# Graph-attention plus relational attention on one core: four reorderings of VectorE and TensorE work

## The chip, the core and the metric

The kernel runs on one core of a Trainium2 chip. A core has a matrix engine (TensorE, "PE" in the profile; its weight loads are listed apart as "PEld"), three engines for elementwise work (VectorE or DVE, ScalarE or ACT, GpSimd or POOL) and SyncE (SP), which here only issues DMAs. Each engine works through its own list of instructions in order and waits on semaphores for the others. The metric is the device time of one execution in microseconds (us).

## The reference

The input is `x` of shape (64, 256, 256), float32: 64 graphs of 256 nodes with 256 features, and `adj`, (64, 256, 256), int32. Two layers follow each other. Everything is float32.

```python
# layer 0: two graph attentions, then a feed-forward block
def _gat(h, adj, W, a, out_features):
    Wh = jnp.matmul(h, W)
    Wh1 = jnp.matmul(Wh, a[:out_features])
    Wh2 = jnp.matmul(Wh, a[out_features:])
    e = Wh1 + jnp.swapaxes(Wh2, 1, 2)
    e = jax.nn.leaky_relu(e, negative_slope=ALPHA)
    scores = jnp.where(adj > 0, e, NEG)
    att = jax.nn.softmax(scores, axis=1)
    return jnp.matmul(att, Wh)
...
h = _gat(x, adj, W1, a1, Fout)
h = _gat(h, adj, W2, a2, W2.shape[1])
h = _layernorm(residual + h, g_ln1, b_ln1)
ff = jnp.matmul(jax.nn.relu(jnp.matmul(h, w_ff1) + b_ff1), w_ff2) + b_ff2
return _layernorm(residual2 + ff, g_ln2, b_ln2)

# layer 1: attention of 8 heads with 32 features each, values by relation, then feed-forward
scores = jnp.einsum('bhid,bhjd->bhij', q, k) / np.sqrt(dh)
attn = jax.nn.softmax(scores, axis=-1)
for r in range(Wv.shape[0]):
    v_r = (src @ Wv[r] + bv[r]).reshape(Bb, Nn, h, dh).transpose(0, 2, 1, 3)
    mask = (adj_matrix == r)[:, None]
    out = out + jnp.einsum('bhij,bhjd->bhid', attn * mask, v_r)
x = _ln(src + attn_out, g1, beta1)
ff = jax.nn.gelu(x @ W1 + b1, approximate=False) @ W2 + b2
return _ln(x + ff, g2, beta2)
```

The hidden width of both feed-forward blocks is 1024.

## The kernel before

Two graphs form a group (512 rows), and the 64 graphs are 32 groups. After a prologue (weights are folded, the first two groups' graph attention and the first feed-forward block of group 0 are done), `turn(u, u+1, u+2)` runs for u = 0 to 31. One turn interleaves three groups at different places of the pipeline: `Y` (group u) does its relational attention and its second feed-forward block, `X` (group u+1) its first feed-forward block, `Z` (group u+2) both graph attentions. Turns 30 and 31 have no `Z`, turn 31 has no `X` either.

Inside `tc.manual_schedule` the engines named there take their instructions in the order in which the Python code emits them: TensorE, SyncE, VectorE and ScalarE in turns with an `X`, TensorE and SyncE alone in turn 31 and in the prologue. GpSimd's order, and what is not named, is left to a scheduler. PSUM, the accumulator that TensorE writes, has eight banks: six are handed out in turn by `bank`, and two ("po", "zo") hold sums of the attention and, earlier in the turn, products of the values.

Large matrix products are split in quarters and done with seven products in place of eight. In each of them the results 1 and 2 go to one quarter of the output, 6 and 3 to another, 5 and 7 to the third, and 4 to the last. What comes first for a quarter is copied out of PSUM by ScalarE, what comes second is added by VectorE. Products 2, 5, 3 share one bank, each on top of the last, and 1, 6, 7, 4 another. So each product waits until the copy or addition of the one before it in its bank has read the bank. There are three of these:

- `Projections` (called as `p("q2 v2 ...")`): queries and keys ("q") and values ("v") of the attention. Copies stand at line 1036, additions at line 1040.
- `hidden_seven` (called as `first("6a")` or `second("2a 1a")`): the 1024 hidden features. Each step is done for two halves, a and b. Products stand at line 898 (tiles h1a and h1b), copies at 907, additions at 910, the activation functions at 916 (steps c, d, s and 4) and 941 (step r). The first product of the second operand needs differences of the input, `tt`, line 881.
- `HiddenOut` (called as `out(1)`): back to 256 features, added into the rows `y`. `product` (line 987, tile yf) and `add` (line 995) can be called apart. `sums` (line 973, tiles eq and eaq) makes the sums of hidden features that products 5, 6, 3 and 7 take.

The names that matter in a turn, in the order of the code:

- `scores`, `powers`, `masks`, `totals` and `sums` do the attention in four parts (two graphs by two sets of four heads). `scores` is the product (tile sp, line 1073), `powers` the exponentials (line 1082, tile e), `masks` multiplies them by the relation's mask (line 1086, tile ea, two instructions of 1024 columns), `totals` adds over a block (line 1091, tile es), and `sums` runs the products po and zo (lines 1101, 1104). zo needs es.
- `normed_features` turns normalised rows into features: four transpositions of 32x32 blocks on VectorE (line 694, tile yt), then sixteen moves across partitions, twelve by DMA and four by GpSimd (lines 711 and 713, or 703; tile hT).
- `early(z)` transposes the rows of group u+2 (line 1128, tile xT, one instruction of 1024 columns). Its readers are the products xpp (line 740).
- `norm` takes the moments (lines 826 and 827) and GpSimd's power of -1/2 (lines 837 and 838, tile rs). `offsets` (line 845, tile nm) is VectorE's small product of mean and rs, and `applied_norm` is ScalarE's scaling of the rows (line 855), four instructions for 512 rows. If `applied_norm` gets no list of rows, it calls `offsets` first.
- `Softmax` (tiles s and z) is the graph attention: `scores` (lines 766 and 768), `exp` (771), `masks` (775, two instructions for each graph) and `shares` (779, the reciprocal z). `scaled` (791) needs z. `first_sums` (line 800, tile hpp) follows.
- `divided` (lines 1112 to 1117) divides the attention by its totals; it is called by `shares(b)` of `turn`.

Of the kernel before, what the change touches and what calls it, by code (L numbers as in the profile page):

```python
# [12 lines left out]
ALU = mybir.AluOpType  # L13
# [372 lines left out]
def narrow_path(  # L386
# [482 lines left out]
    def hidden_seven(u, l, hT, w, bi, func, d, tt):  # L869

        a11, a12, a22, s1, s2, s3, s4 = w
        quarter = [[hT[k][:, b * NB:(b + 1) * NB] for b in range(G)] for k in range(KB)]

        def moving(n):
            return tt[:, n * N:(n + 1) * N].rearrange("p (t a r) -> p t a r", t=NB, r=32)

        def sub(n, x_, y_):  # L880
            nc.vector.tensor_tensor(moving(n), x_, y_, ALU.subtract)  # L881

        sub(0, quarter[0][1], quarter[0][0])
# [4 lines left out]
        one, two = ([None, None] for _ in halves)  # L888

        def out(h, o, b):  # L890

            f = o * FB // 2 + 2 * h
            return d["h1"][:, f:f + 2, b * N:(b + 1) * N]

        def product(ps, h, w_, m, first):
            for i in range(2):
                f = 2 * h + i
                nc.tensor.matmul(ps[:, i * N:(i + 1) * N], w_[:, f * P:(f + 1) * P], m,  # L898
                                 start=first and i == 0, stop=True,
                                 skip_group_check=True)  # L900

        def pair(ps):
            return ps.rearrange("p (f n) -> p f n", f=2)

        def copied(h, o, b, ps):

            mark["copied"] = nc.scalar.copy(out(h, o, b), pair(ps))  # L907

        def added(h, o, b, ps):
            mark["added"] = nc.vector.tensor_tensor(out(h, o, b), pair(ps), out(h, o, b), ALU.add)  # L910

        def done(h, o, b, ps=None):
            for i in range(2):
                f = o * FB // 2 + 2 * h + i
                y = d["h1"][:, f, b * N:(b + 1) * N]
                nc.scalar.activation(y, y if ps is None else ps[:, i * N:(i + 1) * N], func,  # L916
                                     bias=bi[:, f:f + 1])

        def step(name):
            n, h = name[0], "ab".index(name[1])  # L920
            if n == "2":
                two[h] = bank(f"h1b{u}_{l}_{h}")
                product(two[h], h, a12, quarter[1][0], True)
                copied(h, 0, 0, two[h])
            elif n == "1":
                one[h] = bank(f"h1a{u}_{l}_{h}")
                product(one[h], h, a11, quarter[0][0], True)
                added(h, 0, 0, one[h])
            elif n == "5":
                product(two[h], h, s1, moving(0), True)  # L930
                copied(h, 1, 1, two[h])
                mark["fifth"] = mark["copied"]
            elif n == "3":
                product(two[h], h, s4, quarter[1][1], False)
                added(h, 0, 1, two[h])
            elif n == "6":
                product(one[h], h, s2, moving(1), False)
                copied(h, 0, 1, one[h])
            elif n == "r":
                for f in range(2 * h, 2 * h + 2):  # L940
                    nc.scalar.activation(d["h1"][:, f, :], d["h1"][:, f, :], func, bias=bi[:, f:f + 1])
            elif n == "7":
                product(one[h], h, s3, moving(2), False)
                added(h, 1, 1, one[h])
# [61 lines left out]
    class Projections:  # L1006
# [3 lines left out]
        def __init__(s, u, hT):  # L1010
            s.u = u
            s.qk = work.tile([P, KB, 2, TN], F32, tag="q", name=f"qk{u}", bufs=1)
            s.v = work.tile([P, T, 2 * F], F32, tag="v", name=f"v{u}", bufs=1)
            s.h = [[hT[k][:, b * N:(b + 1) * N] for b in range(G)] for k in range(KB)]
            s.one, s.two = {}, {}

        def sums(s):
            tt = work.tile([P, HPB, NB * N], F32, tag="e", name=f"tq{s.u}").rearrange("p a n -> p (a n)")
# [13 lines left out]
            tag = ("zo", "po")[n]  # L1032
            return psum.tile([P, 512], F32, tag=tag, name=f"v{n}_{s.u}")

        def copied(s, x, o, b, ps):
            nc.scalar.copy(s.out(x, o, b), ps.rearrange("p (i n) -> p i n", i=2))  # L1036

        def added(s, x, o, b, ps):
            y = s.out(x, o, b)
            mark["projected"] = nc.vector.tensor_tensor(y, ps.rearrange("p (i n) -> p i n", i=2), y, ALU.add)  # L1040

        def step(s, x, n):
            a11, a12, a22, s1, s2, s3, s4 = wqks if x == "q" else wvs
# [9 lines left out]
                nc.tensor.matmul(ps[:, i * N:(i + 1) * N], l, r, start=n in (1, 2, 5) and i == 0, stop=True,  # L1053
                                 skip_group_check=True)
            to = {1: (0, 0), 2: (0, 0), 5: (1, 1), 6: (0, 1), 3: (0, 1), 7: (1, 1), 4: (1, 0)}[n]
            (s.added if n in (1, 3, 7) else s.copied)(x, *to, ps)

        def __call__(s, names):
            for n in names.split():
# [155 lines left out]
    def turn(y_, x_, z):  # L1215
# [46 lines left out]
        with order:  # L1262
            p.sums()
            if X:
                n = X.pop("n")
                offsets(*n)
            p("q2 v2 q1 v1")
            if X:
                applied_norm(X["y"], *n, [0, 1, 2, 3])
                X["hT"] = normed_features(x_, 0, X["y"])  # L1270
            p("q5")
            scores(0, (0, 1))
# [5 lines left out]
            p("v5 q6")  # L1278
            powers(0, (2,))
            p("v6")  # L1280
            powers(0, (3,))
            if X:
                masks(0)
            p("q3 q7")
            p("v7")
            if X:
                totals(0)
            else:
                with behind("projected"):
                    masks(0)  # L1290
                    totals(0)
            p("v3 q4 v4")
            steps = first_hidden(x_) if X else None
            if waiting:
                last = norm(w, 3, wy, mv=last)
# [3 lines left out]
                offsets(*last)  # L1299
            masks(1, (2,))  # L1300
            totals(1)
            if Z:
                early(z)
            sums(0)
            if waiting:
                first("2a 1a")
                applied_norm(wy, *last, [0, 1])
                first("5a")
                applied_norm(wy, *last, [2, 3])
            else:  # L1310
                first("2a 1a 5a", 1)
            scores(2)
            sums(1)
            first("6a")
# [55 lines left out]
            if Z:  # L1370
                out(1)
                Z["m"].scores(0)
                Z["m"].scores(1)
                Z["m"].exp(0)
                Z["m"].exp(1)
                out.sums(4)
                out(2, 5)
            elif X:
                out(5)
                out.sums(3)  # L1380
            applied_norm(y, *n)
# [42 lines left out]
            second("2a 1a")  # L1424
            if X:
                n = norm(x_, 1, X["y"], mv=n, rest=range(NB + 1, T))
            second("2b 1b ca 6a")
            if X:
# [3 lines left out]
            second("5a")  # L1432
            if X:
                applied_norm(X["y"], *n, [1])
            if Z:
                affine(y, rg3, rb3)
            second("6b 5b cb")
            if Z:
                X["hT"] = normed_features(x_, 1, X["y"], natural=True)
            second("7a 7b sa sb 3a da 3b db 4a 4b")  # L1440
            if X and not Z:
                affine(y, rg3, rb3)
                X["hT"] = with_ones(to_features(X["y"], f"h2T{x_}", (nc.vector.tensor_copy,) * 2))
            if y_ >= NG - 2:
                pieces = out_pieces(y_, y, h1)
                if X:
# [36 lines left out]
    with tc.manual_schedule(engines={mybir.EngineType.PE, mybir.EngineType.SP}):  # L1483
# [90 lines left out]
```

## Time and profile before

| | |
|---|---|
| median of three runs | 3062.04 us (3059.02 to 3063.88) |
| the profiled execution | 3056.92 us |
| its span, first to last instruction | 3055.3 us |
| mean granted TensorE clock | 0.994 of full speed |
| SyncE's DMA queue q1 | 418,076 packets, 102.20 MB, 15.3% of 16 engines |

A turn (but the last, 85 us) takes 91 to 95 us, measured from one group's first projection difference to the next one's. In the 40 slices of the profile TensorE is at 90% or more in all but the first and the last. A matmul in the trace overlaps the next one, so a busy TensorE row hides short waits; the rows of the weight loads (PEld) show them. In these lines, the number in brackets is the idle time of the engine before the first instruction of the row, with what ended it. The chain of waits gives, for each piece, its start, its length and its place; the table of waits gives who waited for whom, the sum in us, how often, and the longest.

### The profile page before, as it was taken

The page shows a single profiled execution, that of the slowest core. Times are in us where ns is not written, and L with a number is a line of the kernel's source. Part 1 is how long each engine was busy: PE and PEld are TensorE (multiplying, and loading weights), DVE is VectorE, ACT ScalarE, POOL GpSimd, SP SyncE. Part 2 cuts the span into 40 slices and gives each one's busy share as a digit, 9 for nine tenths or more (in the row PEclk, how much of TensorE's full clock was granted, in tenths as well). Part 3 has the DMA queues.
Part 4 walks back from the last instruction along what each step waited for, and adds up shares of the span by engine and source line. Part 5 has one row for each costly group of instructions (what it writes and reads, how often), then busy time and mean ns, then how long its engine had stood idle before and what let it go on. Part 6 is the DMA issues. An engine that isn't in the chain of part 4 may idle for free.

```text
span 3055.3 us, 58545 instructions
## 1 busy us (share of the span) xinstructions
PE 2966.2 (97%) x22192; PEld 2496.0 (82%) x22192; DVE 2614.3 (86%) x5025; ACT 1718.4 (56%) x3562; POOL 638.3 (21%) x930
## 2 busy tenths in 40 slices
PE   7999999999999999999999999999999999999997
PEld 5788888888888888888888888888888887888876
DVE  4788888889888889898889888898888888988876
ACT  4455555655655655555556556555556555555553
POOL 4222111221211222211222212222112212112211
PEclk8999999999999999999999999999999999999999
DMA  5011111211111211111111112111112111111000
GB/s 147 13 31 39 37 38 25 44 37 39 37 33 32 44 37 39 34 27 41 42 37 39 34 25 44 37 40 37 39 25 44 37 39 34 28 39 37 24 8 16
DMA packets 428405, 113.26 MB, mean 37 GB/s; under 512 B 364587, under 2 KB 427605, under 8 KB 428117
## 3 DMA queue, kind: packets, MB, share of 16 engines
q1 hardware_dynamic: 418076, 102.20, 15.3%
q10 hardware_dynamic: 8984, 6.19, 0.8%
q8 instruction: 178, 2.92, 0.4%
q0 software_dynamic: 1056, 1.05, 0.1%
q14 instruction: 111, 0.90, 0.1%
HBM read 56.78 MB, written 16.78 MB: 24 GB/s over the span
## 4 chain that ended last, share of the span: by engine, by line
PE 67%; DVE 17%; SPq 6%; DMA 3%; POOL 3%; issue 2%; ACT 1%; ACTq 0%; DVEq 0%; POOLq 0%
PE yf L987 21%; PE h1a L898 13%; PE h1b L898 9%; SPq L713 6%; PE po L1101 4%; PE xpp L740 4%; PE yop L811 4%; PE ygp L811 3%; DVE yt L694 3%; PE qk L1053 2%; DMA hT<-yt 2%; PE v L1053 2%; DVE s L775 2%; DVE tt L881 2%; PE sp L1073 1%
## 5 line engine op out<-in xcount | busy, mean ns | idle before, releaser
L1086 DVE TENSOR_TENSOR ea<-e,aT 128x1024 f32<-128x1024 f32 x256 | 308.0, 1215 | 54.5 <-ACT e L1082 54.5
L855 ACT ACTIVATE y<-y,nm,rs 128x256 f32<-128x256 f32 x450 | 242.6, 593 | 163.0 <-DVE nm L845 158.3
L1082 ACT ACTIVATE e<-sp 128x512 f32<-128x512 f32 x512 | 270.5, 597 | 27.7 <-PE sp L1073 21.0
L907 ACT COPY h<-h1b 128x512 f32<-128x512 f32 x256 | 149.0, 582 | 214.2 <-PE h1b L898 206.3
L837 POOL TENSOR_SCALAR rs<-mv 128x4 f32<-128x4 f32 (+1 forms) x134 | 56.3, 420 | 963.7 <-DVE mv L827 833.7
L1036 ACT COPY qk<-qk 128x512 f32<-128x512 f32 x128 | 74.5, 582 | 317.0 <-PE qk L1053 316.9
L916 ACT ACTIVATE h<-h,cols 128x256 f32<-128x256 f32 x512 | 222.3, 502 | 36.7 <-DVE h L910 36.7
L711 POOL COPY hT<-yt 32x256 f32<-32x256 f32 x244 | 207.4, 850 | 151.2 <-DVE yt L694 140.1
L826 DVE BATCH_NORM_STATS2 st<-y 128x6 f32<-128x256 f32 x512 | 208.3, 409 | 5.5
L995 DVE TENSOR_TENSOR y<-yf,y 128x256 f32<-128x256 f32 x448 | 185.2, 414 | 27.2 <-PE yf L987 27.0
L910 DVE TENSOR_TENSOR h<-h1a,h 128x512 f32<-128x512 f32 x256 | 170.0, 677 | 35.5 <-PE h1a L898 31.6
L1114 POOL TENSOR_TENSOR low<-low,rq 128x16 f32<-128x16 f32 x64 | 13.9, 217 | 755.4 <-DVE rq L1113 755.4
L867 DVE TENSOR_TENSOR y<-y,rb 128x1024 f32<-128x1024 f32 (+1 forms) x130 | 167.0, 1285 | 3.2
L864 DVE TENSOR_TENSOR y<-y,rg 128x1024 f32<-128x1024 f32 (+1 forms) x130 | 161.7, 1244 | 1.2 <-ACT y L855 1.1
L1091 DVE TENSOR_TENSOR es<-e 128x1024 f32<-128x1024 f32 x128 | 156.0, 1219 | 0.0
L742 ACT COPY xp<-xpp 128x260 f32<-128x260 f32 x128 | 45.5, 386 | 195.4 <-PE xpp L740 195.3
L838 POOL TENSOR_TENSOR rs<-rs,mhalf 128x4 f32<-128x4 f32 (+1 forms) x134 | 146.5, 1094 | 8.3
L1073 PE MATMUL sp<-qk 32*128 32x256 f32 x2048 | 146.6, 400 | 0.0
L1101 PE MATMUL po<-e,v 128*32 128x256 f32 x2048 | 136.3, 384 | 0.0
L1101 PE MATMUL po<-ea,v 128*32 128x256 f32 x2048 | 135.9, 379 | 0.0
L987 PEld LDWEIGHTS yf<-wf,eaq 128*128 128x128 f32 x1024 | 119.1, 192 | 16.3 <-DVE eaq L973 15.0
L740 PE MATMUL xpp<-gwe,xT 128*128 128x260 f32 x512 | 128.7, 396 | 3.8 <-ACT xT L675 3.8
(284 smaller groups left out, 7670.1 us busy)
## 6 DMA issues: line engine op xcount, KB each, us to landing
hT<-yt SPq DMA_DIRECT2D x912, 32.0 KB, 1.9
y<-in_x_dram SPq DMA_DIRECT2D x32, 512.0 KB, 4.8
xq<-in_x_dram SPq DMA_DIRECT2D x240, 64.0 KB, 2.2
aq<-in_adj_dram SPq DMA_DIRECT2D x240, 64.0 KB, 2.4
out_dram<-y SPq DMA_DIRECT2D x30, 512.0 KB
hT<-yt ACTq DMA_DIRECT2D x180, 32.0 KB, 1.8
wf<-in_L_gnn_w_ff_dram SPq DMA_DIRECT2D x2, 1024.0 KB, 7.5
w<-in_L_gnn_W_dram SPq DMA_DIRECT2D x2, 1024.0 KB, 7.4
```

The costliest lines, as they stand in the source:

```text
L711: nc.gpsimd.tensor_copy(to, at)
L740: nc.tensor.matmul(ps[:, :WX], hT[k][:, t * P:(t + 1) * P], gwe[:, k, :], start=(k == 0), stop=(k == KB - 1))
L811: nc.tensor.matmul(ps[:, i * F:(i + 1) * F], lhs(t, k), rhs(b, k), start=(k == 0), stop=(k == n - 1))
L826: nc.vector.bn_stats(st[:, t, :], y[:, t, :])
L855: mark["normed"] = nc.scalar.activation(y[:, t, :], y[:, t, :], AF.Identity, bias=nm[:, t:t + 1], scale=rs[:, t:t + 1])
L898: nc.tensor.matmul(ps[:, i * N:(i + 1) * N], w_[:, f * P:(f + 1) * P], m, start=first and i == 0, stop=True, skip_group_check=True)
L916: nc.scalar.activation(y, y if ps is None else ps[:, i * N:(i + 1) * N], func, bias=bi[:, f:f + 1])
L987: nc.tensor.matmul(s.ps[n][:, i * F2:(i + 1) * F2], a[:, k, i * P:(i + 1) * P], w_[:, k, :], start=n in (1, 2, 5) and i == 0 and k == 0, s ...
L995: mark["out"] = nc.vector.tensor_tensor(yq, s.ps[n][:, :F].rearrange("p (i f) -> p i f", i=NB), yq, ALU.add)
L1082: nc.scalar.activation(e[:, a, :], ps[a], AF.Exp, scale=isd)
L1086: nc.vector.tensor_tensor(ea[:, a:a + 2, :], e[:, a:a + 2, :], ab[:, None, :].to_broadcast([P, 2, NB * N]), ALU.mult)
L1101: nc.tensor.matmul(po[hp, m * N:(m + 1) * N], vs[:, hp], w[:, a, j * N:(j + 1) * N], start=(n == 0), stop=(n == len(terms) - 1))
```

## The change

Nothing is computed differently and no instruction of a middle turn is added or removed. For the turns in the middle (1 to 29; the first item also in turn 30) VectorE's order changes in three places, and TensorE's, SyncE's and ScalarE's orders stay:

1. Projections: the second of the two mask instructions of attention part 0 moves behind the additions of q3 and q7 and stays ahead of that of v7.
2. `early(z)`, the transposition xT, moves behind the steps "2a 1a 5a" of the first feed-forward block, so on VectorE behind the addition of 1a (turn 0 too).
3. While group u's rows are normalised for its second feed-forward block (turns 0 to 29): `offsets` comes first, then addition 2, one graph's masks, addition 5, the other's masks, the reciprocal. Addition 6 moves behind the four transpositions (product 6 stays where it was), and addition 3 behind sum 3.

In the turns at both ends, products are done in another order: `hidden_seven` in the first feed-forward block of group 0 and in the second one of turns 30 and 31 goes 2 1 5 3 6 7 4 in place of 2 1 6 5 7 3 4 (halves alternating), and the projections of turns 0 and 31 do v5 q3 v3 q6 v6 q7 v7 q4 v4 in place of v5 q6 v6 q3 q7 v7 v3 q4 v4. Turn 30 normalises all four row blocks on ScalarE, where GpSimd did two of them, and moves the transposes into the next group's features ahead of the steps "sa sb 4a 4b". The helpers `copied` and `added` become one, `taken`, which copies a quarter's first product and adds its second, whichever comes first.

```diff
+        def taken(h, o, b, ps):
+            if (h, o, b) in begun:
+                mark["added"] = nc.vector.tensor_tensor(out(h, o, b), pair(ps), out(h, o, b), ALU.add)
+            else:
+                begun.add((h, o, b))
+                mark["copied"] = nc.scalar.copy(out(h, o, b), pair(ps))
...
-            p("q2 v2 q1 v1")
+            middle = X and y_
+            p("q2 v2 q1 v1" if middle else "q1 v1 q2")
...
             if X:
-                masks(0)
-            p("q3 q7")
-            p("v7")
+                masks(0, (0,))
+            if middle:
+                p("q3 q7")
+                masks(0, (2,))
+                p("v7")
+            else:
+                p("q6 v6 q7 v7")
+                if X:
+                    masks(0, (2,))
...
-            p("v3 q4 v4")
+            p("v3 q4 v4" if middle else "q4 v4")
...
             totals(1)
-            if Z:
-                early(z)
             sums(0)
...
                 first("2a 1a 5a", 1)
+            if Z:
+                early(z)
             scores(2)
...
                 out.sums(4)
-                out(2, 5)
+                offsets(*n)
+                out(2)
+                applied_norm(y, *n, range(T))
+                Z["m"].masks(0)
+                out(5)
+                Z["m"].masks(1)
+                Z["m"].shares()
...
-            applied_norm(y, *n)
-            if Z:
-                Z["m"].masks(0)
-                Z["m"].masks(1)
-                Z["m"].shares()
+            if not Z:
+                applied_norm(y, *n)
+            else:
                 Z["m"].scaled(WH)
...
-            if X:
+            if Z:
+                out.product(6)
+                hT = normed_features(y_, 2, y, queues=(nc.sync, nc.scalar))
+                out.add(6)
+                out.sums(3)
+                out(3)
+            elif X:
                 out(6)
-                if not Z:
-                    out.sums(4)
-                if Z:
-                    hT = normed_features(y_, 2, y, queues=(nc.sync, nc.scalar))
-                    out(3)
-                    out.sums(3)
-                else:
-                    out(7, 3)
+                out.sums(4)
+                out(7, 3)
...
+            else:
+                if X:
+                    n = norm(x_, 1, X["y"], mv=n, rest=range(NB + 1, T))
+                second("2a 1a 2b 1b")
+                second("5a 5b")
+                if X:
+                    applied_norm(X["y"], *n)
+                second("3a 3b 6a 6b ca cb da db 7a 7b")
+                if X:
+                    affine(y, rg3, rb3)
+                    X["hT"] = with_ones(to_features(X["y"], f"h2T{x_}", (nc.vector.tensor_copy,) * 2))
+                second("sa sb 4a 4b")
...
-        first_hidden(0)("2a 1a 2b 1b 6a 5a 6b 5b 7a 7b sa sb 3a ra 3b rb 4a 4b")
+        first_hidden(0)("2a 1a 2b 1b 5a 5b 3a 3b 6a ra 6b rb 7a sa 7b sb 4a 4b")
```

More of the change, by code (lines that the diff above doesn't have):

```diff
@@ L888, in hidden_seven @@
         one, two = ([None, None] for _ in halves)
+        begun = set()
         def out(h, o, b):
@@ L903, in pair @@
             return ps.rearrange("p (f n) -> p f n", f=2)
[L905 to L910, printed above, removed]
+        def taken(h, o, b, ps):
[4 more added lines that the diff above has]
+                mark["copied"] = nc.scalar.copy(out(h, o, b), pair(ps))
         def done(h, o, b, ps=None):
@@ L923, in step @@
                 product(two[h], h, a12, quarter[1][0], True)
-                copied(h, 0, 0, two[h])
+                taken(h, 0, 0, two[h])
             elif n == "1":
@@ L927, in step @@
                 product(one[h], h, a11, quarter[0][0], True)
-                added(h, 0, 0, one[h])
+                taken(h, 0, 0, one[h])
             elif n == "5":
                 product(two[h], h, s1, moving(0), True)
-                copied(h, 1, 1, two[h])
+                taken(h, 1, 1, two[h])
                 mark["fifth"] = mark["copied"]
@@ L934, in step @@
                 product(two[h], h, s4, quarter[1][1], False)
-                added(h, 0, 1, two[h])
+                taken(h, 0, 1, two[h])
             elif n == "6":
                 product(one[h], h, s2, moving(1), False)
-                copied(h, 0, 1, one[h])
+                taken(h, 0, 1, one[h])
             elif n == "r":
@@ L943, in step @@
                 product(one[h], h, s3, moving(2), False)
-                added(h, 1, 1, one[h])
+                taken(h, 1, 1, one[h])
             elif n in "cds":
@@ L1014, in __init__ @@
             s.h = [[hT[k][:, b * N:(b + 1) * N] for b in range(G)] for k in range(KB)]
-            s.one, s.two = {}, {}
+            s.one, s.two, s.begun = {}, {}, set()
         def sums(s):
@@ L1033, in bank, with taken @@
             return psum.tile([P, 512], F32, tag=tag, name=f"v{n}_{s.u}")
[L1035 to L1040, printed above, removed]
+        def taken(s, x, o, b, ps):
+            y, ps = s.out(x, o, b), ps.rearrange("p (i n) -> p i n", i=2)
+            if (x, o, b) in s.begun:
+                mark["projected"] = nc.vector.tensor_tensor(y, ps, y, ALU.add)
+            else:
+                s.begun.add((x, o, b))
+                nc.scalar.copy(y, ps)
         def step(s, x, n):
@@ L1055, in step @@
             to = {1: (0, 0), 2: (0, 0), 5: (1, 1), 6: (0, 1), 3: (0, 1), 7: (1, 1), 4: (1, 0)}[n]
-            (s.added if n in (1, 3, 7) else s.copied)(x, *to, ps)
+            s.taken(x, *to, ps)
         def __call__(s, names):
@@ L1266, in turn @@
                 offsets(*n)
-            p("q2 v2 q1 v1")
+            middle = X and y_
+            p("q2 v2 q1 v1" if middle else "q1 v1 q2")
+            if middle:
+                applied_norm(X["y"], *n, [0, 1, 2, 3])
+            elif X:
+                applied_norm(X["y"], *n, [0])
+            if not middle:
+                p("v2")
+            if X and not middle:
+                applied_norm(X["y"], *n, [1])
+            if not middle:
+                p("q5")
+            if X and not middle:
+                applied_norm(X["y"], *n, [2, 3])
             if X:
-                applied_norm(X["y"], *n, [0, 1, 2, 3])
                 X["hT"] = normed_features(x_, 0, X["y"])
-            p("q5")
-            scores(0, (0, 1))
+            if middle:
+                p("q5")
+                scores(0, (0, 1))
+            else:
+                scores(0, (0,))
+                p("v5")
+                powers(0, (1,))
             if z + 1 < NG:
@@ L1277, in turn @@
                 last = moments(w, 3, wy, range(NB))
[L1278 to L1281, printed above, removed]
-            if X:
-                masks(0)
-            p("q3 q7")
-            p("v7")
+            p("v5 q6" if middle else "q3 v3")
+            if middle:
+                powers(0, (2,))
+                p("v6")
+                powers(0, (3,))
+            else:
+                powers(0, (2, 3))
+            if X:
+                masks(0, (0,))
+            if middle:
+                p("q3 q7")
+                masks(0, (2,))
+                p("v7")
+            else:
+                p("q6 v6 q7 v7")
+                if X:
+                    masks(0, (2,))
             if X:
@@ L1380, in turn @@
                 out.sums(3)
-            applied_norm(y, *n)
-            if Z:
-                Z["m"].masks(0)
-                Z["m"].masks(1)
-                Z["m"].shares()
+            if not Z:
+                applied_norm(y, *n)
+            else:
                 Z["m"].scaled(WH)
                 nc.scalar.activation(work.tile([P, 1], F32, tag="ve", name=f"ve{y_}"), mhalf[:, 0:1], AF.Gelu)
-            if X:
-                out(6)
-                if not Z:
-                    out.sums(4)
-                if Z:
-                    hT = normed_features(y_, 2, y, queues=(nc.sync, nc.scalar))
-                    out(3)
-                    out.sums(3)
-                else:
-                    out(7, 3)
+            if Z:
[4 more added lines that the diff above has]
+                out(3)
+            elif X:
+                out(6)
+                out.sums(4)
+                out(7, 3)
             if not Z:
@@ L1423, in turn @@
             h1 = Y["h1"] = work.tile([P, FB, TN], F32, tag="h1", name=f"h1{y_}_1", bufs=1)
-            second("2a 1a")
-            if X:
+            if Z:
+                second("2a 1a")
                 n = norm(x_, 1, X["y"], mv=n, rest=range(NB + 1, T))
-            second("2b 1b ca 6a")
-            if X:
+                second("2b 1b ca 6a")
                 offsets(*n)
@@ L1431, in turn @@
                 applied_norm(X["y"], *n, [2, 3], True)
-            second("5a")
-            if X:
+                second("5a")
                 applied_norm(X["y"], *n, [1])
-            if Z:
                 affine(y, rg3, rb3)
-            second("6b 5b cb")
-            if Z:
+                second("6b 5b cb")
                 X["hT"] = normed_features(x_, 1, X["y"], natural=True)
[L1440 to L1443, printed above, removed]
+                second("7a 7b sa sb 3a da 3b db 4a 4b")
+            else:
+                if X:
[9 more added lines that the diff above has]
+                second("sa sb 4a 4b")
             if y_ >= NG - 2:
```

## The prediction

> **What bounds the kernel now.** I read the busy shares first, then the waits, then the chain that ended last, and last the timeline of one ordinary turn (turn 10, about 1030 to 1122 us).
>
> ```profile
> PE 2966.2 (97%) x22192; PEld 2496.0 (82%) x22192; DVE 2614.3 (86%) x5025; ACT 1718.4 (56%) x3562; POOL 638.3 (21%) x930
> ...
> PE 67%; DVE 17%; SPq 6%; DMA 3%; POOL 3%; issue 2%; ACT 1%; ACTq 0%; DVEq 0%; POOLq 0%
> ```
>
> TensorE looks full, yet a third of the chain runs through other engines: TensorE waits shortly, several times in each turn, for a VectorE queue that is dense just there. The waits name the places:
>
> ```profile
> PEld h1a L898 <- DVE h L910: 38.7, 33, 3.3
> PEld qk L1053 <- DVE qk L1040: 21.6, 31, 0.7
> PEld yf L987 <- DVE eaq L973: 15.0, 30, 0.5
> ```
>
> They are one wait each per turn, and the three parts of the change sit before exactly these. The chain of turn 10 shows which of them count:
>
> ```profile
> 1050.15 1.83 DMA hT<-yt
> ...
> 1058.51 1.14 DVE es L1091
> 1059.65 1.15 DVE xT L1128
> 1060.80 0.59 DVE h L910
> ...
> 1061.43 1.13 PE h1a L898 x4
> ...
> 1089.91 0.42 DVE y L995
> 1090.34 0.07 DVE nm L845
> 1090.41 1.39 DVE s L775 x8
> ...
> 1092.31 1.33 DVE yt L694 x4
> 1093.64 0.31 DVE y L995
> 1093.95 1.29 DVE eaq L973
> 1095.25 0.04 issue
> 1095.29 2.05 PE yf L987 x16
> ```
>
> Chain one: normalised rows are transposed at 1041.71, SP issues twelve moves of 0.59 us, the last lands at about 1052; VectorE then works without a break through es, the row transposition xT and the addition h that step 6a of the hidden product needs. The wait of q4 at 1049.39 is not on this chain: TensorE catches up by standing at 6a. Chain two: from product 5's addition to eaq, which product 7 needs.
>
> **What the Trainium skill says.** "Perfetto Trace Analysis", Identifying the Most-Contended Engine, holds matmul busy time a bad measure and weight loads a better one; the trace agrees (97% against 82%), so I read waits on the PEld rows. Its section What "DMA-bound" means calls a queue of solid issue slices bound by issuing; SP's twelve slices of 0.59 us, 0.04 us apart, are that, and the change leaves them alone. Its section Optimizing Scalar/DVE Operations says that half of a profiled latency lies beside the next instruction: here a 1024-wide mask lasts 1.20 to 1.23 us, but its successor starts 1.15 us after it, a 512-wide addition 0.69 and 0.65. I add up steps, not durations. "TensorE: Matmul & The Clock Gate", What's actually happening, says that an idle window of about 3.4 us halves the clock. The trace agrees at 3019.97, below.
>
> **Part 1, second mask behind the query additions (turns 1 to 30).** VectorE did mask, q3, q7, v7, es, v3; it will do q3, q7, mask, v7, es, v3. q7's product ends at 1047.37, so its addition runs 1047.40 to 1048.06 and q4's load, free at 1048.72, no longer waits until 1049.39. But v7's addition now stands behind the mask: 1048.06+1.15+0.65 = 1049.86, so v4 waits to about 1049.93 instead of 1049.58. TensorE reaches the scores 0.32 us earlier (1051.00 for 1051.32), not 0.67. The last addition, v3, ends as before (1047.40+0.65+1.15+0.65+1.15+0.65 = 1051.65). As 6a is bound by chain one, alone this is worth about nothing.
>
> **Part 2, xT behind the first addition.** In each of turns 1 to 29 I measured from the end of es: 6a's load stands at +1.87 us, and the load before it shows that without the wait it would come 0.36 to 1.16 us sooner (gap 0.77 to 1.57 less the 0.41 that follows every zo group). With the addition first it ends at +0.65; zo's loads (behind es) and their 0.76 us let 6a start at +0.81 at the earliest. 6a thus gains 0.7 us, with part 1 up to 0.97. It doesn't keep it. xT and the addition together take what they took, so all that VectorE does after them keeps its time: the addition of 1b ends at +6.52 in every turn, and 6b, which writes 1b's bank, loads at +6.94:
>
> ```profile
> 1065.40 1.34 DVE L910 TENSOR_TENSOR h<-h1a,h 128x512 f32<-128x512 f32 x2
> 1066.50 0.84 PEld L898 LDWEIGHTS h1a<-tt,wf1s 128*128 128x128 f32 x4
> ```
>
> (The first of the two additions is 1b's, the second 7a's.) So 6b can move from +6.94 to about +6.58. TensorE restarting from a wait has its first matmul with the load instead of 0.22 us after it, and the next load after 0.76 us, not 0.865. The step after 6b, 4a, begins its matmuls at 6.58+0.97 = +7.55 for +8.02: 0.47 us stays. 7a's addition ends at +7.18, before 4a's new load at +7.34. ScalarE's later steps and 3b's addition follow by 0.43 or more, and from there both engines wait for each other, not for a DMA. 29 x 0.47 = 13.6 us. Bounds: 0.37 (no gain from the restart) and 0.97 (no wait at 6b); I take 0.47, since the 0.42 us between addition and load are constant to 0.01 in 29 turns. xT's SP load of the next rows starts 0.65 us later; SP's next work is 30 us off. xT's readers come 10 us later.
>
> **Part 3, offsets ahead (turns 0 to 29).** Counted from the reciprocal z (1091.82 here; all 30 turns agree to 0.02): POOL's rs ends at -3.57, eaq of the fourth sum gives VectorE free at -2.81, the offsets come only at -1.57, behind additions 2 and 5, of which the second waits 0.48 us for TensorE. New order: offsets -2.81, addition 2 -2.75, two masks -2.40 to -1.71, addition 5 (its product ended at about -1.95), two masks, z at -0.55. Then the transpositions at -0.45; their normalised rows are done by ScalarE at -0.54 (it starts 0.19 after the offsets and needs 2.08), so four steps end at about +0.95; addition 6 to +1.26; eaq done at +2.6, where it was +3.41. Product 7 could load at +2.96 and did at +3.46. Its wait goes, with 0.3 us over; by matmul starts the next group moves from 1097.18 to 1096.82: 0.36 us, x 30 = 10.8 us. Addition 3, now behind eaq, is wanted by nobody on TensorE soon: the next group that may want its bank starts at 1096.8, 2 us after it.
> The moves hT<-yt start 0.86 us earlier on SP's queue and, behind ScalarE's scaling and table load, 0.55 us earlier on ScalarE's. In 9 of 30 turns the second hidden product waits for them (0.18 to 2.51 us); there TensorE gains 0.55, not 0.36: 9 x 0.19 = 1.7 us.
>
> **Part 4, ends.** In turns 30 and 31 step 6a stands third in line, long before the addition of 1a is through:
>
> ```profile
> 2952.17 0.73 PEld L898 LDWEIGHTS h1a<-tt,w1s 128*128 128x128 f32 x4 [2.46 <-DVE h L910]
> 3019.97 1.17 PEld L898 LDWEIGHTS h1a<-tt,w1s 128*128 128x128 f32 x4 [3.25 <-DVE h L910]
> ```
>
> 5a 5b 3a 3b need only ScalarE's copies and fill 4 x 0.865 = 3.46 us. In turn 31 the hidden product ends at about 3026 for 3030.2, and the half clock after the wait (loads of 1.17 for 0.84) goes too; then ScalarE's 16 activations bind, from 3020.5 with two copies to about 3028.6, where product 2 began at 3032.05: 3.4 us. In turn 30, 7a now waits for 6a's addition, whose copy stands behind four normalisations on ScalarE (two were POOL's), to about 2957.0; the steps end 0.8 us later, but the transposes to the next projections come two steps earlier, and their copies and the 1.0 us behind them with it: 1.2 us gained. In the first hidden product, which had no wait, 7a and 4a come one step behind the addition they need (about 1.05 us against 0.865), and turn 0 likewise: 1.0 us lost. Sum 3.6; bounds -2 and 7.
>
> **Sum.** 13.6+10.8+1.7+3.6 = 29.7 us. The profiled execution took 3056.9 us (span 3055.3), so 3027.2; the median of the runs is 5.1 us above it: 3032.3.
>
> **Rivals.**
> A, the 6b wait does not come (VectorE reaches 1b earlier than its old order says): 0.97 in place of 0.47, 14.5 us more: 3018. For it: nothing but that other orders around shares could shift; against it: a constant distance. 8%.
> B, one of the two stages gives its gain back to a later wait (3b's addition behind ScalarE's last activation, or scores that wait for banks), and the end turns bring nothing: 29.7-13.6-3.6 = 12.5 us: about 3049. For it: VectorE is dense for 12 us after es; against it: the slacks above. 14%.
> C, slower: the transpositions of the normalised rows are now ahead of addition 6 and of eaq; if ScalarE's last row comes later than VectorE wants it (+0.6), both stand behind it, and product 7 with them. Product 7 reaches its old time when that row comes at +1.45 (1.45+0.35+0.31+1.3 = 3.41), and part 2 is outweighed from +1.9; at +2.5 product 7 is 1.05 us later than before, less the 0.47 of part 2 some 0.58 a turn, 17 us in 30 turns, less 3.6: about 3076. ScalarE would have to be 2.5 to 3 us late, while it is idle 1.81 us before this row today. 4%.
> D, it changes nothing measurable, because the streams wait elsewhere: the built order shows equal instructions in the order described, so only by compensation: 3062. 4%.
>
> **How the numbers follow.** The forecast has 70%, its own range 3024 to 3041. The range 3018 to 3050 takes in A, B and the bounds of part 4. Under 0.2% (6 us, about what runs that spread over 4.9 us can tell) counts as no change. Faster 91%, same 5%, slower 4%.
>
> **What would show it.** Right: the waits of h1a and yf on DVE gone in the middle turns, a new wait of h1a at 6b on the 1b addition of 0.5 to 0.6 us, a short one of v on v7's addition, the turn shorter by 0.8 us, the 2.46 and 3.25 us waits gone. Wrong: 6a still waiting, 6b not, or yt waiting for ScalarE.

## The result, and the profile after

| | before | changed | 
|---|---|---|
| median of the runs taken side by side | 3062.96 us (3059.02 to 3064.6, 4 runs) | 3021.6 us (3020.98 to 3023.5, 4 runs) |
| the profiled execution | 3056.92 us | 3021.42 us |
| its span | 3055.3 us | 3019.7 us |

The ratio is 0.9868, 95% interval 0.9851 to 0.9885: 41 us faster, where 30 were forecast. The profiled executions differ by 35.5 us. (The profiled execution of before lies 6 us under the median and below each of its timed runs, the lowest of which took 3057.5 us; these 6 us of the 41 can't be looked for in the pair of traces.)

The first two lines of the page to compare, busy time and the chain by engine:

```profile
PE 2965.3 (98%) x22192; PEld 2492.9 (83%) x22192; DVE 2609.3 (86%) x5025; ACT 1729.2 (57%) x3564; POOL 642.9 (21%) x928
...
PE 76%; DVE 13%; SPq 4%; issue 2%; DMA 2%; POOL 2%; ACT 1%; ACTq 0%; DVEq 0%; POOLq 0%
```

Busy times are the same to 0.2% on TensorE and VectorE, in a span 35.6 us shorter: nothing became cheaper, waits went. On the chain, TensorE has 76% for 67%, VectorE 13% for 17%, and the share of transfers fell.

Of the three waits shown before (who waited for whom, sum in us, times, longest), those of qk on its additions and of yf on eaq are gone or down to six; these two are there now:

```profile
PEld h1a L899 <- DVE h L908: 35.8, 65, 2.3
...
PEld v L1055 <- DVE v L1039: 9.8, 30, 0.3
```

The first looks as if nothing was won at h1a: 35.8 us for 38.7. But it is now 65 waits, not 33: in each middle turn a gap of 0.41 us ahead of 6a, which stands after every zo group, and a new one of 0.75 us (median of 29) ahead of 6b. The second is the new wait of v4 behind the mask. The timeline of turn 10 has both sides of it (start, length, engine and line; the bracket is the idle time before):

```profile
1048.44 1.22 DVE L1093 TENSOR_TENSOR es<-e 128x1024 f32<-128x1024 f32 x1
...
1049.57 0.69 DVE L908 TENSOR_TENSOR h<-h1a,h 128x512 f32<-128x512 f32 x1
...
1050.17 1.24 DVE L1130 STREAM_TRANSPOSE xT<-xq 128x1024 f32<-128x1024 f32 x1
1050.58 0.73 PEld L899 LDWEIGHTS h1a<-tt,wf1s 128*128 128x128 f32 x4 [0.41 <-DVE h L908]
...
1055.42 1.28 DVE L908 TENSOR_TENSOR h<-h1a,h 128x512 f32<-128x512 f32 x2
1056.15 0.73 PEld L899 LDWEIGHTS h1a<-tt,wf1s 128*128 128x128 f32 x4 [0.53 <-DVE h L908]
1056.90 0.84 PEld L899 LDWEIGHTS h1a<-tt,wf 128*128 128x128 f32 x4
```

Count from 1049.57, the end of es: 6a loads at +1.01 (it was +1.87), but 6b at +6.58 and 4a at +7.33. The chain of the same turn runs through exactly this: from 1047.30 on it is VectorE for 8.8 us (1.7 of them are listed as issue; the timeline has VectorE at a division and a mask there), and TensorE again from 6b:

```profile
1047.30 1.22 DVE ea L1088
1048.52 1.14 DVE es L1093
...
1055.42 0.69 DVE h L908
...
1056.15 1.99 PE h1a L899 x8
```

The moves hT<-yt, which headed this piece of the chain before, are no longer in it. At the other place the chain has no VectorE left: from 1074.06 to 1090 it is TensorE alone. The timeline shows why:

```profile
1078.56 0.15 DVE L845 SCALAR_TENSOR_TENSOR nm<-mv,rs 128x4 f32<-128x4 f32 x1
...
1080.79 0.18 DVE L779 RECIPROCAL z<-z 128x4 f32<-128x4 f32 x1
1080.89 1.39 DVE L694 STREAM_TRANSPOSE yt<-y 128x256 f32<-128x256 f32 x4
...
1082.51 1.36 DVE L974 TENSOR_TENSOR eaq<-h 128x1024 f32<-128x1024 f32 x1
...
1084.36 1.75 PEld L988 LDWEIGHTS yf<-wf,eaq 128*128 128x128 f32 x14
```

Product 7 loads at 1084.36 with no bracket; eaq is through about 0.5 us earlier.

### The profile page after: what moved, and what is told of

It is laid out like the page before. It is cut to its first block, busy times and chain, and to the rows that moved or that the text cites. A ratio compares the mean times of both kernels' runs of the same rounds, so it can differ in the third digit from the quotient of the medians.

```text
span 3019.7 us, 58579 instructions
## 1 busy us (share of the span) xinstructions
PE 2965.3 (98%) x22192; PEld 2492.9 (83%) x22192; DVE 2609.3 (86%) x5025; ACT 1729.2 (57%) x3564; POOL 642.9 (21%) x928
## 4 chain that ended last, share of the span: by engine, by line
PE 76%; DVE 13%; SPq 4%; issue 2%; DMA 2%; POOL 2%; ACT 1%; ACTq 0%; DVEq 0%; POOLq 0%
PE yf L988 25%; PE h1a L899 12%; PE h1b L899 8%; PE po L1103 5%; SPq L713 4%; PE v L1055 4%; PE qk L1055 4%; PE xpp L740 4%; PE yop L811 4%; PE hpp L800 3%; PE ygp L811 3%; PE sp L1075 2%; DVE ea L1088 2%; DVE h L908 2%; PE zo L1106 1%
## 5 line engine op out<-in xcount | busy, mean ns | idle before, releaser
L899 PE MATMUL h1a<-tt,wf 128*128 128x256 f32 x512 | 131.3, 380 | 0.0
```

## The experiments

For each kernel the stretches of a turn are compared, as means over turns 1 to 29 in us: from the first projection load to the fourth scores (A), from there to product 7 (B), to 2a of the second hidden product (C), and to the next turn's first projection (D). The fourth scores are `scores(3)` in the code; the expectations, which count from zero, call them the third. "Ratio" is to before, measured on the same chip.

| kernel | median us | ratio, 95% interval | A | B | C | D | turn |
|---|---|---|---|---|---|---|---|
| before | | | 33.35 | 25.03 | 5.57 | 28.59 | 92.54 |
| changed | 3021.6 | 0.9868 (0.9851 to 0.9885) | 32.90 | 24.55 | 5.54 | 28.57 | 91.57 |
| e1 part 1 alone | 3061.8 | 0.9997 (0.9990 to 1.0003) | 33.32 | 25.03 | 5.63 | 28.58 | 92.56 |
| e2 part 2 alone | 3048.5 | 0.9948 (0.9936 to 0.9961) | 32.89 | 25.03 | 5.70 | 28.69 | 92.31 |
| e3 part 3 alone | 3042.7 | 0.9931 (0.9918 to 0.9944) | 33.37 | 24.55 | 5.57 | 28.57 | 92.06 |
| e4 ends alone | 3055.4 | 0.9973 (0.9962 to 0.9984) | 33.34 | 25.03 | 5.62 | 28.62 | 92.61 |
| e5 changed, no part 1 | 3022.2 | 0.9868 (0.9850 to 0.9886) | 32.91 | 24.55 | 5.51 | 28.54 | 91.51 |
| e6 changed, additions as before | 3032.0 | 0.9897 (0.9881 to 0.9914) | 32.91 | 24.84 | 5.63 | 28.55 | 91.93 |
| e7 xT later still | 3028.4 | 0.9886 (0.9870 to 0.9903) | 32.39 | 25.20 | 5.58 | 28.57 | 91.75 |
| e8 e7, second mask later | 3023.5 | 0.9871 (0.9850 to 0.9892) | 32.27 | 25.19 | 5.55 | 28.58 | 91.59 |
| e9 e7, es later | 3033.7 | 0.9898 (0.9883 to 0.9913) | 32.41 | 25.16 | 5.76 | 28.58 | 91.91 |
| e10 both | 3028.3 | 0.9879 (0.9864 to 0.9894) | 32.26 | 25.17 | 5.77 | 28.63 | 91.83 |
| e11 changed, offsets as before | 3064.3 | 1.0005 (0.9996 to 1.0013) | 32.86 | 24.70 | 6.48 | 28.84 | 92.86 |
| e12 e11, last move on SP | 3027.5 | 0.9879 (0.9862 to 0.9896) | 32.89 | 24.70 | 5.53 | 28.60 | 91.72 |

### Each part by itself: e1 to e4

e1 is before with the second mask of part 0 behind q3 and q7:

```diff
-                masks(0)
+                masks(0, (0,) if y_ else (0, 2))
                 p("q3 q7")
+            if X and y_:
+                masks(0, (2,))
```

> The kernel before with part 1 alone (second mask behind the additions of q3 and q7, turns 1 to 30). My theory: no change of time, 0 +-3 us of some 3060, because step 6a stays bound by the DMA chain (es, xT, addition 1a): the wait of q4 (0.70 us idle of the weight loads) goes, one of v4 on v7's addition of about 0.3 us comes, and the gap before 6a grows by 0.32 us in every turn. Rival (each wait of TensorE that goes is time won): 29 x 0.32 = 9 us faster.

1.1 us less, an interval that holds 1. The wait of q4 went, v4's of 0.33 us came, and the gap ahead of 6a grew from a median of 1.13 to 1.49 us: TensorE arrives 0.36 us sooner and stands 0.36 us longer.

e2 is before with `early(z)` moved behind the steps "2a 1a 5a":

> The kernel before with part 2 alone (xT behind the first addition, turns 0 to 29). My theory: 0.47 us a turn, 13.6 us faster, whatever the gap before 6a was: 6a 0.7 us earlier, but 6b then waits for 1b's addition and loads at +6.57 from the end of es, 4a at +7.33. Rival (the whole wait of 6a is won): median 0.72 us a turn, 21 us faster, and no wait at 6b.

14.4 us less. In the trace stretch A loses 0.46 us a turn, 13.2 us in 29; C and D together are 0.23 us longer than in the profiled execution of before, which is the low one. 6b loads at +6.58 in this kernel too, and its wait appears in 23 of 29 turns.

e3 is before with part 3: offsets first, addition 5 between the masks, additions 6 and 3 later.

> The kernel before with part 3 alone (offsets ahead, additions 6 and 3 behind; turns 0 to 29). My theory: 0.36 us a turn and a little for the moves hT, 11 to 13 us faster; the gap of product 7 of 0.50 us gone, z 0.57 us earlier. Rival (VectorE is 0.6 to 0.8 us earlier there, and so is the DMA that the next product waits for): 0.6 us a turn, 18 us.

20.2 us less. Stretch B gives 0.47 a turn. The traces have 14 us between them, since the execution of before that was profiled is itself 6 us below its median; in which stretch these 6 us lie isn't settled.

e4 is the changed kernel with the three parts undone: before with the new order of products in turns 0, 30, 31 and the first hidden product, turn 30's new normalisation, and `taken`:

> The changed kernel with the three parts undone in the middle turns, so the kernel before with the new product order in the first hidden product and in turns 0, 30 and 31. After the trace of the changed kernel: 0.7 us lost ahead of turn 0, about 1.5 won in turn 0 (q1 and v1 start before GpSimd has set the row of ones), 0.7 in turn 30 and 4.4 in turn 31: 6 us faster. As forecast before the result: 3.6 us. Rival (the ends are worth nothing beyond the noise, and what the total holds above the forecast is run-to-run scatter of the kernel before): 0 us.

7.5 us less, twice what I had for it. In the trace turn 0 is 1.56 us shorter and the last stretch 4.43 us (both counted from a turn's first projection difference, a VectorE instruction); the middle turns are as before, to 0.07 us a turn.

The four add up to 1.1 + 14.4 + 20.2 + 7.5 = 43.2 us, for 41.4 of the whole change. The parts hardly touch each other, with one question left: does part 1 earn something once 6a no longer waits? e5 is the changed kernel with the mask back ahead of q3 in the middle turns:

```diff
-                masks(0, (0,))
+                masks(0, (0, 2) if middle else (0,))
                 if middle:
                     p("q3 q7")
-                    masks(0, (2,))
```

> The changed kernel with part 1 undone in the middle turns (both masks ahead of the additions of q3 and q7 again). My theory: the stretch from the first projection to the third scores is the same as in the changed kernel or at most 0.05 us longer, 0 to 2 us in all: 6a loads up to 0.4 us later (at +1.1 to +1.5 from the end of es where it is not held by es), but 6b at +6.58 as before, bound by 1b's addition. Rival (once parts 2 and 3 are in, TensorE is the bound, and part 1 is worth its 0.32 us): 9 us slower than the changed kernel.

The ratio is 0.9868 again. What comes earlier at 6a is spent ahead of 6b; part 1 is worth nothing in either company.

### Part 3 taken apart: e6, e11 and e12

e6 is the changed kernel with additions 6 and 3 at their old places, so only the offsets come early:

```diff
-                out.product(6)
+                out(6)
                 hT = normed_features(y_, 2, y, queues=(nc.sync, nc.scalar))
-                out.add(6)
+                out(3)
                 out.sums(3)
-                out(3)
```

> The changed kernel with additions 6 and 3 at their old places (6 ahead of the four transpositions, 3 ahead of sum 3); the offsets stay ahead. Theory: product 7 does not wait (eaq done about 0.3 us later, 0.17 us of room left), so the stretch from the third scores to product 7 stays at 24.55 us, and only the moves hT begin about 0.3 us later: 2 to 4 us slower through the turns in which the hidden product waits for them. Rival (the two additions' places are what removes the wait of product 7): the stretch goes back towards 24.9 us, 10 us slower.

10 us slower than the changed kernel. VectorE came to addition 6 before TensorE had product 6 ready, and the transpositions stood behind it:

```profile
1080.88 0.42 DVE L996 TENSOR_TENSOR y<-yf,y 128x256 f32<-128x256 f32 x1 [0.27 <-PE yf L988]
1081.22 1.41 DVE L694 STREAM_TRANSPOSE yt<-y 128x256 f32<-128x256 f32 x4
...
1084.28 1.86 PEld L988 LDWEIGHTS yf<-wf,eaq 128*128 128x128 f32 x16 [0.32 <-DVE eaq L974]
```

I had taken it that with early offsets product 7 would wait for nothing. It does wait, 0.31 us in each of 30 turns. An addition moved behind work that is ready takes away a hole in VectorE's row, which I had not counted.

e11 is the other half: additions late, offsets back behind additions 2 and 5.

```diff
-                offsets(*n)
                 out(2)
+                out(5)
+                offsets(*n)
                 applied_norm(y, *n, range(T))
                 Z["m"].masks(0)
-                out(5)
```

> The changed kernel with the offsets at their old place (behind additions 2 and 5), additions 6 and 3 at the new ones: the other half of part 3. Theory: the transpositions and sum 3 come 0.31 us earlier each than in the kernel before, so product 7 waits 0.14 us instead of 0.50: stretch from the third scores to product 7 about 24.7 us (25.03 before, 24.55 in the changed kernel, 24.84 with the offsets alone), 3 to 6 us slower than the changed kernel. Rival (only both together free product 7): 24.9 us or more, 10 us slower.

Stretch B came out at 24.70, with product 7 waiting 0.17 us. Yet the kernel is as slow as before: 2a of the second hidden product waits in each of turns 0 to 29, 33.6 us in all (9.0 before, 4.5 in the changed kernel). Its input hT is read 1.3 us later after z than before (median), although the transpositions end 0.3 us earlier after it. The chain of one turn shows one move waiting for another:

```profile
634.75 2.06 DMA hT<-yt
...
636.84 2.62 DMA hT<-yt
...
639.81 1.10 PE h1b L899 x4
```

The records of these instructions name the semaphore that each transfer counts up and the one that its issue waits for (times in us):

```
e11      SP    move 5           634.753  waits $S[114]   counts 114
         SP    output, 512 KB   636.393
         ACT   move 6           636.837  waits $S[114]   counts 114
changed  ACT   move 1           623.955  counts 114
         ACT   move 6           627.901  waits $S[114]   counts 114
         SP    output, 512 KB   628.378
```

The transfers of both queues go through eight completion semaphores in turn, in one order over both queues that the scheduler sets, and one that takes a semaphore again is not issued until its last user has landed: in 25 of the 29 middle turns of e11 the sixth move starts 0.02 us after the last count of the fifth's landing. In e11 five moves of SP stand ahead of ScalarE's first one, in the changed kernel four. So ScalarE's sixth move shares with SP's fifth, which is still under way, in place of ScalarE's first, long landed. It starts 0.93 us late (mean of 24 turns; in the other five ScalarE's fifth move was late already), behind the output's 512 KB write, and the reader of hT starts 2.9 us after it, for 2.2 us in those 25 of 29 turns of the changed kernel in which the write comes after the move. The Trainium skill, "DMA: Bandwidth & Descriptors", Issuing engines are not separate DMA queues, says that transfers started by different engines run on the same 16 DMA engines and interleave; this trace agrees as far as the move's later landing behind SP's write goes.

e12 is e11 with this one move on SP, as its seventh:

```diff
-                hT = normed_features(y_, 2, y, queues=(nc.sync, nc.scalar))
+                hT = normed_features(y_, 2, y, queues=(nc.sync, nc.scalar) * 5 + (nc.sync,) * 2)
```

> The kernel of e11 (additions 6 and 3 late, offsets at their old place) with one thing changed: the sixth ScalarE move hT<-yt of the second hidden product is issued on SP's queue, as its seventh. In the trace of e11 the sixth ScalarE move starts 6.38 us after the reciprocal z, 0.93 us after ScalarE could issue it, because it shares its completion semaphore with SP's fifth move and waits until that has landed (in the other traces it shares with the first ScalarE move, long landed). By then SP has issued the 512 KB write of the output (5.94), and the last move lands behind it, 2.9 us after its issue start, for 2.2 in the other traces. My theory: this shared semaphore, not the order of VectorE, made e11 lose. Then hT is whole at about +8.2 in place of +9.56, the second hidden product waits as seldom as before (stretch from product 7 to it 5.6 in place of 6.48 us), the next one (28.84) goes back to 28.6, and the kernel takes 1.1 us a turn less than e11: about 3064 - 29 x 1.1 = 3032, within 3028 to 3042. Rival one: the moves are late because the offsets and with them ScalarE's normalisations and scalings are late, so a seventh move on SP doesn't help: 3064, stretch 6.4. Rival two: the seventh move on SP is itself late, because SP needs 0.6 us for each and shares the engines with the write: half of it, 3048.

37 us less than e11 (3027.5; ratio to before 0.9879, 0.9862 to 0.9896); C falls from 6.48 to 5.53 and D from 28.84 to 28.60. Neither rival is left: the normalisations are as late as in e11 (ScalarE ends them 0.70 us after z in both), and the seventh SP move is not too late. One move cost e11 37 us. In the trace of the same turn the output's write comes behind the moves, and tt follows after 0.51 us:

```profile
632.50 0.54 SPq L1193 DMA_DIRECT2D out_dram<-y  x1
633.84 0.43 DVE L881 TENSOR_TENSOR tt<-hT 128x256 f32<-128x256 f32 x1 [0.51 <-DMA hT<-yt]
```

With e12 part 3 can be divided: of its 0.47 us in stretch B the late additions bring 0.33 (25.03 to 24.70), the offsets' new place the last 0.14; the offsets alone, in e6, 0.19.

### Beyond the change: e7 to e10

6b waits because VectorE does xT before 1b's addition. e7 moves `early(z)` behind "2b ra 1b 7a", past both additions:

```diff
-            if Z:
-                early(z)
             scores(2)
...
             first("2b ra 1b 7a")
+            if Z:
+                early(z)
             masks(2, (2,))
```

> The changed kernel with xT moved further, behind the additions of 1b and 7a and ahead of the second mask of attention part 2. My theory (xT ahead of 1b's addition is what holds 6b and gives half of the gain back): no gap before 6b, which loads at about 5.07 us after 6a; 0.5 us a turn more, some 14 us faster than the changed kernel, about 3007. Rival (another wait stands right behind it: 4a for 7a's addition, 3b's addition for ScalarE, or the scores for banks): 0 to 4 us faster, with a new gap at that place.

6b's wait went and stretch A lost the 0.51 us foreseen, but B gained 0.65. xT now stands ahead of a mask and es, 3b's addition comes behind all three, and ScalarE's activation, the exponentials and the banks that they empty come behind that:

```profile
1058.49 1.23 DVE L1130 STREAM_TRANSPOSE xT<-xq 128x1024 f32<-128x1024 f32 x1
...
1060.75 1.21 DVE L1093 TENSOR_TENSOR es<-e 128x1024 f32<-128x1024 f32 x1
...
1061.89 0.68 DVE L908 TENSOR_TENSOR h<-h1b,h 128x512 f32<-128x512 f32 x1
...
1062.60 1.34 ACT L942 ACTIVATE h<-h,cols 128x512 f32<-128x512 f32 x2 [1.48 <-DVE h L908]
...
1064.47 0.74 PEld L740 LDWEIGHTS xpp<-gwe,xT 128*128 128x128 f32 x4 [0.80 <-ACT e L1084]
```

e8 adds to e7 that the second mask goes behind v7's addition too:

> As the run before, and the second mask of attention part 0 behind v7's addition too. Theory: the gap of v4 (0.33 us) goes, 6a comes up to 0.25 us earlier in those turns where it is not held by es at +0.74: some 3 us faster than the run before. Rival (chain one, the twelve moves of SP, holds all of it): no difference.

A loses another 0.12 us, the xpp wait stays, and the kernel is level with the changed one (intervals 0.9850 to 0.9892 and 0.9851 to 0.9885).

e9 is e7 with es out of 3b's way:

```diff
-            totals(2)
-            first("3b rb 7b")
+            first("3b rb")
+            totals(2)
+            first("7b")
```

> The changed kernel with xT behind the additions of 1b and 7a (as in e7) and the sum es of attention part 2 moved from ahead of 3b's addition to behind it. In e7 the gain to the third scores came (0.51 us a turn), and 0.65 us were lost right after, because 3b's addition came behind xT and es, with it ScalarE's step rb, the exponentials behind that, and the bank that the second product xpp waits for. Theory: with es out of the way 3b's addition is 0.7 us earlier, xpp does not wait, the stretch to product 7 is 24.55 to 24.6 us again, to the third scores 32.4: some 14 us faster than the changed kernel, 3007. Rival (the turn is full at this place: what VectorE does not do before, it does after, and something else waits, as po for the last masks): as the changed kernel, 3022, or slower.

The xpp wait went, and one of the same size came two products later, at yop (the output product of the attention), in all 30 turns:

```profile
1075.95 1.59 PEld L811 LDWEIGHTS yop<-wo,qk 128*128 128x128 f32 x8 [0.74 <-ACT xp L742]
1075.98 1.97 PE L811 MATMUL yop<-wo,qk 128*128 128x256 f32 x8 [0.37 <-DVE qk L1119]
```

The loads' row names ScalarE's copy, but that ends at 1076.03, after the first load; the matmuls' row names the division qk, which is through at 1075.83 (1075.14 + 0.69). VectorE has no idle time between es (1063.44) and this division, so whatever is pushed back into that piece comes due at the division. e10 has both edits:

> As the run before, and the second mask of attention part 0 behind v7's addition. Theory: 0.12 us a turn more, as e8 had over e7 in the stretch to the third scores, 3.5 us: about 3004. Rival: no difference.

3028.3 us. A + B is 57.43 here, 57.45 in the changed kernel, 57.59 in e7, 57.46 in e8 and 57.57 in e9. The sum hardly moves while its two terms trade 0.6 us. That e9 takes 5 us more than e7 at the same sum lies in C (5.76 for 5.58): 2a of the second hidden product waits 9.5 us over the middle turns in e9's trace, 4.2 in e7's; the same wait is 9.4 us in e10 and 3.2 in e8. Why these waits differ was not looked into. None of these kernels beats the changed one.

## Why the prediction held, point by point

The three places were named rightly, with their sizes for parts 1 to 3. The timed 3021.6 us lies within 3018 to 3050, but under the forecast's own 3024 to 3041, and by the total alone nearer to rival A's 3018 than to 3032.3; the wait at 6b decides against A. The miss of 10.7 us has two halves. Between the profiled executions 5.8 us more were gained than forecast, in two terms below. The other 4.9 us are the last step of the sum, which carried the 5.1 us between the profiled execution of before and its median over to the changed kernel: there the two are 0.2 us apart.

- **Part 1 about nothing.** Shown twice, alone (e1) and with the others (e5). The 0.33 us that v4 was to lose is what the wait table has.
- **Part 2, 0.47 us a turn, bound by 1b's addition.** Measured 0.46 in the trace, 14.4 us timed for 13.6. The positions came out as the working had them: 1b's addition ends at +6.52, 6b loads at +6.57 (predicted +6.58), 7a's addition ends at +7.12 (+7.18), 4a loads at +7.33 (+7.34). They were sums of VectorE's steps, not of its durations. Rival A needed 6b not to wait; it waits in all 29 turns.
- **Part 3, product 7.** The offsets come 2.23 us before z (predicted 2.26: at -2.81, with the new z at -0.55), ScalarE's rows are through at +0.03 and the transpositions start at +0.09, so rival C's late row never came. 0.36 us a turn were forecast; stretch B gives 0.47 and C's shortest value takes 0.11 back (5.31 to 5.42): 0.36.
- **Part 3, the moves: the term that was too small.** 1.7 us were put down for hT, from 0.55 us earlier on ScalarE's queue in 9 turns. ScalarE's scalings had not been waiting for z alone, but for ScalarE's own normalisations, which ended 0.70 us after z. With the offsets first they start 0.21 after z in place of 0.60, and z is itself 0.57 earlier: 0.96 us. hT is read 0.87 us earlier (least distance from the start of the fourth sum's eaq: 10.87 for 11.74). The share of stretch C above its least value fell from 0.26 to 0.12 us, 4.0 us in 29 turns between the two traces (5.7 if before is averaged with e1, e2 and e4, and the changed kernel with e3 and e5). e11 and e12 show how much more this term can weigh.
- **The ends: also too small, 3.6 for 7.5.** Turns 30 and 31 are 5.1 us shorter, for 4.6 forecast: in turn 31 5a 5b 3a 3b filled the 3.25 us wait as foreseen, and the last stretch is 4.36 us shorter for 3.4, turn 30 0.74 for 1.2 (each counted from the first projection difference). The start, forecast to cost 1.0 us, gained 2.4. The loss in the first hidden product can't be read from this pair: from its first load to the second group of products behind it, four traces with the old order have 17.5 to 19.0 us, ten with the new one 18.1 to 19.2. Missed was turn 0: I had its new order cost like the prologue's, but turn 0 is 3.06 us shorter (1.56 with the ends alone, e4; over the traces it takes 86.9 to 90.9 us with the new order and 90.9 to 91.7 with the old). The edits at the ends were not run one by one, so what each of them brings is read from traces only. The table of waits before has one more line, of GpSimd, that I had read past:

```profile
PEld qk L1053 <- POOL h2T L686: 9.1, 2, 5.4
```

  Turn 0's products q2 v2 waited 5.40 us for the row of ones that GpSimd writes late. The new order begins with q1 v1, which don't read that half of the features: they run from 103.49 on, and q2 waits 2.48 us. (The other of the two waits, 3.65 us, stood at turn 31's first projection; 1.64 us are left there.)
- **The sum.** Profiled: 13.0 (A) + 10.5 (B and C's least value) + 4.0 (hT) + 0.5 (D) + 7.5 (the ends and turn 0, its share of part 3 with it) = 35.5, as between the executions, for 29.7 forecast. The last 6 us of the timed gain are the low execution of before; no trace shows where they lie.

## What to carry to other kernels

On an engine that works through a dense queue, a reordering moves a wait to the next customer: look for who comes second, add up the steps to it, and count only the difference (here 0.46 us, where the first customer's load came 0.86 us sooner in turn 10). Put what has to wait for another engine behind what is ready; late additions brought more than the early start of the chain that looked critical (0.33 to 0.14 us). After any reordering see whether transfers that share a completion semaphore have changed partners, since that cost 37 us in e11, nearly all that the change gains.

## What the runs showed of the hardware

- A move of 32 KB takes about 0.6 us to issue on SP's queue and lands 1.9 us after the issue starts (medians). Its reader started 2.2 to 2.3 us after the start of the last issue, and 2.9 to 3.4 us after it where the 512 KB write had been issued first (means over such turns in each of fourteen traces; e11 has none of the first kind).
- A wait on a transfer's semaphore sits on the queue of the issuing engine: in e11 ScalarE's copies of hpp stand behind the sixth move, 637.39 for an issue that ended at 637.35. The Trainium skill, "DMA: Bandwidth & Descriptors", Anatomy of one DMA — SWDGE (gpsimd) path, puts any wait for a semaphore on the issuing sequencer, before dispatch; that section is about transfers of GpSimd, and the trace shows the same on ScalarE's queue.
- ScalarE's queue issues transfers while its arithmetic goes on: the first move of that turn of e11 is issued at 631.97, while the activation of ve, which stands before it in the code, starts only at 634.06.
